# A macaron block on one core: block 2's down sum of the first FFN in sixteen steps, with six of the first attention round's scores between them

## The chip, the cores and the metric

The kernel runs on one core of one Trainium2 chip. A core has five engines, each with its own instruction queue: TensorE (PE, matrix products; its loading of weights is shown as PEld), VectorE (DVE), ScalarE (ACT), GpSimd (POOL) and SyncE (SP), which here only issues DMA transfers. PE writes its results to PSUM, from where DVE and ACT fetch them. The metric is the device time of one execution in microseconds; the time given for a kernel is the median over runs.

## What is computed

The reference is a macaron block over x of 2 sequences of 1024 tokens with 256 channels: half an FFN, attention, half an FFN again, each on a layer norm of x and added to x.

```python
x = x + 0.5 * ffn(layernorm(x), w_gate, w_up, w_down)
x = x + attn(layernorm(x), Wq, bq, Wk, bk, Wv, bv, Wo, bo)
x = x + 0.5 * ffn(layernorm(x), w_gate, w_up, w_down)

def ffn(x, w_gate, w_up, w_down):
    h = silu(x @ w_gate) * (x @ w_up)          # 1024 hidden
    h = keep_the_2_largest_of_each_4(h)        # by absolute value
    return h @ w_down
```

The attention has 32 query heads of size 8 on 8 key heads, rotary positions, a causal mask and a softmax.

## The kernel before

**Blocks and units.** The 2048 tokens are cut into four blocks of 512 (0 to 3; blocks 0 and 1 are the first sequence). The first FFN goes block by block: a layer norm and transpose, gate and up products (`gate_up`, L252), DVE's masks for the 2-of-4 choice (`mask`, L275 to L292, the last of which writes h), and the down sum. The down sum of a block (`down_half`, L297 to L316) is two halves of two tiles with eight matmuls each, 32 matmuls in all; the profile shows two records for each of them. The generator yields after every second matmul, so that a block has 16 steps of two matmuls. `down` runs a whole half per step of the plan; `down_slowly` gives the steps singly. A finished half is added to x either by DVE (`add`, L340) or by ACT and POOL (`add_aside`, L329 and L330).

Attention goes over 16 units, one for each sequence and key head. A unit's operands are made by `prepare`: PE transposes (hT, L529), ACT copies the result to stage (L537), and DMAs spread it into the tiles qT and kT (L550, L557) on rows that were cleared or set to one earlier. Only unit 0 uses the queues of SP and ACT, all others use SP alone. A unit is then worked in two passes. The first (`pass1`, L584 for the scores, L599 for the mask on the diagonal, L613 for DVE's maxima) finds the row maxima; they are split in two numbers by POOL (L415, L416), transposed (mT, L640), and copied by DMA into qT (L651). The second (`pass2`, L669) makes the scores once more, already shifted by the maxima, ACT takes the exponent (L679), POOL clears what lies above the diagonal (L685), and `weighted` (L706) multiplies with the values. A round interleaves the second pass of one unit with the first pass of the next; round 0 has the first pass of unit 0 only, 18 scores.

**Order.** The engines' order is written by hand where it matters. `run` follows a plan, a string of steps; PE's and DVE's instructions are issued just so. In it g is a group of gate and up products, m a part of a mask, d a half of a down sum, a an addition, l a part of a layer norm, and p one step of the attention's generator, which projects the first sequence and prepares unit 0. Rounds follow the string `order`; there PE and POOL keep the written order, and the other engines are ordered by a scheduler. PE executes in its written order: an instruction that waits holds up those behind it.

The plan of the first FFN ends with block 2's down sum and its two additions. Then the attention's generator goes on: it opens new pools in the space that the first FFN used, and clears there the qT and kT of two more units (`rows`, L397 and L400), which waits for that FFN's last readers. Round 0 follows, and beside its scores block 3's down sum, in steps of `down_slowly`: two steps at each odd one of the first twelve scores, and what is left at the end of the round. The score tiles are taken from `ps_big`, which has three buffers that go round among gate and up products, transposes hT and scores of both passes. The sums take one buffer of `ps_acc` and one of `ps_tr`; the latter serves mT too.

Of the kernel before, what the change touches and what calls it, by code (L numbers as in the profile page):

```python
# [35 lines left out]
def macaron_kernel(  # L36
# [23 lines left out]
    ps_tr = ctx.enter_context(tc.tile_pool(name="ps_tr", bufs=1, space=PSUM))  # L60
    ps_acc = ctx.enter_context(tc.tile_pool(name="ps_acc", bufs=1, space=PSUM))
# [161 lines left out]
    class FFN:  # L223
# [79 lines left out]
        def down_half(self, tb, t2, pool, tag):  # L303
# [11 lines left out]
                        yield  # L315
            self.adds.append((tb, t2, o))  # L316

        def down_slowly(self, tb):

            for t2 in range(2):  # L320
                yield from self.down_half(tb, t2, ps_acc, "acc")
                self.add_aside()
# [26 lines left out]
        def run(self, plan, gens, outs=()):  # L349

            make = {"g": self.gate_up, "d": self.down}
            with tc.manual_schedule(engines={mybir.EngineType.PE, mybir.EngineType.DVE}):
                for op in plan.split():
                    if op == "m":
                        if next(self.masks[0], 0) == 0:
                            self.masks.pop(0)
                    elif op == "a":
                        self.add()  # L360
                    elif op == "o":
                        if next(outs[0], 0) == 0:
                            outs.pop(0)
                            next(outs[0])
                    else:
                        if op not in gens:
                            tb = int(op[1])
                            gens[op] = (
                                make[op[0]](tb)
                                if op[0] in make  # L370
                                else layernorm_T(tb, lambda tb=tb: self.normed(tb), halves=tb == 0)
                            )
                        next(gens[op])

# [9 lines left out]
    def attention(actx, beside_first, beside_last, outs):  # L386
# [413 lines left out]
        def parsed(order):  # L800
            return [(op[0], *map(int, op[1:])) for op in map(str.split, order.split(";"))]

        ops = parsed(order)
        PAIRS = [("av", k) for k in (1, 3, 5, 7)]
        first = max(i for i, op in enumerate(ops) if op[0] == "p1" and op[1] < 3)
        units = [(b, g) for b in range(B) for g in range(NKV)]
# [4 lines left out]
        def step(op, prev, cur, nxt):  # L811
            kind, *arg = op
            if kind == "p1" and cur is not None:
                cur.pass1(*steps1[arg[0]], arg[1:] or (0, 1))
            elif kind == "p2" and prev is not None:
                es = prev.pass2(*steps2[arg[0]], arg[1:] or (0, 1))
                made.setdefault(arg[0], (prev, {}))[1].update(es)
            elif kind == "av" and arg[0] in made:
                unit, es = made.pop(arg[0])
                qh, kbs = steps2[arg[0]]  # L820
                last = arg[0] in (2, 9)
                unit.weighted(qh, kbs, es, last)
                if last and unit.g == NKV - 1:
                    outs.append(output(unit.b, qh))
                    next(outs[-1])
                    if unit.b < B - 1:
                        divisions.append(outs[-1])
            elif kind == "neg1" and prev is not None:
                prev.negated(1)
            elif kind == "shift":  # L830
                unit = prev if arg[0] == 1 else cur
                if unit is not None:
                    unit.shift(arg[0])
            elif kind == "prep" and nxt is not None:
                nxt.prepare()
# [5 lines left out]
        prev, cur = None, Unit(*units[0])  # L841
        cur.prepare()
        yield
        rctx = ExitStack()
        right = rctx.enter_context(tc.tile_pool(name="att2r", bufs=1, side="right"))
        rows(right)
# [7 lines left out]
        def a_step():  # L854
            while beside and next(beside[0], beside) is beside:
                beside.pop(0)

        def round_(n, prev, cur):
            nxt = Unit(*units[n + 1]) if n + 1 < len(units) else None
            if n == 1:  # L860
                beside.append(second)
            if nxt is not None and nxt.b == 1:
                for _ in second:
                    pass
            firsts = 0
            for i, op in enumerate(ops):
                step(op, prev, cur, nxt)
                if i == first and cur is not None:
                    cur.negated(0)
                if n == 0 and i == first:  # L870

                    nc.scalar.activation(warm, cur.maxima[0][:, 0, 6:7], AF.Exp, scale=0.0)
                if n == 0 and op[0] == "p1":
                    firsts += 1
                    if firsts <= 12:
                        for _ in range(2 * (firsts % 2)):
                            next(beside_first, None)
                if n > 0:
                    for _ in range(2 if op in PAIRS else op[0] in ("av", "prep")):
                        a_step()  # L880
                if n > NKV and op == ("av", 5) and divisions:
                    next(divisions.pop(0))
            return cur, nxt

        engines = {mybir.EngineType.PE, mybir.EngineType.Pool}
        with tc.tile_pool(name="att_round0", bufs=2, side="right") as late["2"]:
            with tc.manual_schedule(engines=engines):
                prev, cur = round_(0, prev, cur)
                for _ in beside_first:
                    pass  # L890
# [6 lines left out]
        with tc.manual_schedule(engines=engines):  # L897
            for n in range(1, len(units)):
                prev, cur = round_(n, prev, cur)
# [11 lines left out]
    with ExitStack() as fctx:  # L911
        actx = ExitStack()
        gens, outs = {}, []

        def second_starts():


            while not second:
                yield
            made = [outs.pop(0), outs.pop(0)]  # L920
            lns = [
                layernorm_T(tb, lambda tb=tb: second[0].normed(tb), copy=nc.vector.tensor_copy)
                for tb in range(2)
            ]

            for k in (0, 1):
                next(made[k])
            yield
            for gen in (made[0], made[0], lns[0], made[1], made[1], lns[0], lns[1], lns[0]):
                next(gen)  # L930
                yield
            for gen in (lns[1], lns[1]):
                next(gen)
                yield

        second = []
        with last_units:
            first = FFN(0, False, f0 := ExitStack(), wd_sb, last_pool)
            att = attention(actx, first.down_slowly(NTB - 1), second_starts(), outs)
            with f0:  # L940
                first.run(
                    """
                    l0 l0 l0 l1 g0 l1 g0 l2 g0 g0 l2 g0 m l1 g0 g0 l2 m g0 m g1 m g1 m g1 m
                    g1 g1 m g1 d0 m a d0 l3 a p g1 p g1 m g2 m p g2 m g2 m p p p g2 p d1 m m
                    g2 m d1 a a l3 g2 p g2 l3 p g2 m p g3 p p m g3 p p m g3 g3 g3 m g3 m g3
                    m g3 p m m m d2 d2 a a
                    """,
                    {"p": att},
                )
            next(att)  # L950
        next(att)
        early_ctx.close()
        second.append(FFN(1, True, fctx))
        for _ in att:
            pass
        second[0].run(
            """
            o g0 g0 g0 g0 m o g0 g0 o m g0 o g0 m g1 m g1 m g1 m g1 o g1 l2 g1 d0 m l2 g1 g1
            m m m l2 a d0 g2 m g2 o g2 g2 o m a g2 m o l3 g2 l3 g2 d1 m m g2 m m l3 d1 g3 m
            g3 g3 g3 a a g3 m g3 m g3 m g3 d2 m m m a d2 d3 a d3 a a  # L960
            """,
            gens,
            outs,
        )
        actx.close()
# [56 lines left out]
```

## Time and profile before

| what | us |
|---|---|
| median of 3 runs | 820.93 (820.42 to 822.25) |
| profiled execution, its own time | 824.67 |
| span of the profiled execution | 822.9 |
| PE busy (matmul) | 786.1, 96% of the span |
| DVE busy | 654.7, 80% |
| ACT busy | 426.9, 52% |
| POOL busy | 236.2, 29% |
| L613, DVE's maxima of scores, 288 of them | 343.2 |
| L307, PE's down sums, 512 records | 116.6 |

The span is the time from the first to the last recorded instruction, the profiled execution's own time contains what lies around it. Busy time is a mean over stages that are bound by different engines, so the stretch in which the change lies has to be read by itself: it reaches from about 166 us, where block 2's down sum begins, to about 211 us, where round 1 begins. Matmul records overlap, as they are pipelined: the time of a row of records is read from the start of the first to the start of what follows. The granted clock of PE is given as a share of full speed.

### The profile page before, as it was taken

How to read it: one execution, taken by the hardware profiler on the slowest of the kernel's cores; microseconds unless marked ns; L12 is line 12 of the kernel's file. 1: busy time of each engine (PE TensorE's matmuls, PEld its weight loads, DVE VectorE, ACT ScalarE, POOL GpSimd, SP SyncE). 2: the span in 40 equal slices, each digit the busy share in tenths (PEclk: the TensorE clock that was granted, in tenths of full speed). 3: DMA queues.
4: the chain of work that ended last, by engine and by line, in shares of the span. 5: the costliest groups of instructions: out<-in, count | busy, mean ns of one | idle time of the engine just before them, and what ended most of it. 6: DMA issues, size and time to landing. Idle time of an engine off the chain costs nothing.

```text
span 822.9 us, 13949 instructions
## 1 busy us (share of the span) xinstructions
PE 786.1 (96%) x5344; PEld 426.4 (52%) x5344; DVE 654.7 (80%) x871; ACT 426.9 (52%) x531; POOL 236.2 (29%) x443
## 2 busy tenths in 40 slices
PE   5999999998899999999999999999999999999998
PEld 2447574476544444454444444444445445657466
DVE  4797999898768796888888788888885479788692
ACT  1331313211677776877787687878877423122210
POOL 3000294821265465464222322233223100000000
PEclk9999999999999999999999899999999999999999
DMA  8100000022213222311333323322202200000001
GB/s 276 31 0 2 0 2 0 0 41 41 33 27 64 44 46 50 67 31 44 66 68 70 93 65 68 56 44 51 57 28 92 74 1 16 1 26 1 11 16 51
DMA packets 31010, 36.03 MB, mean 44 GB/s; under 512 B 12896, under 2 KB 20960, under 8 KB 30944
## 3 DMA queue, kind: packets, MB, share of 16 engines
q1 hardware_dynamic: 29118, 31.85, 17.2%
q10 hardware_dynamic: 1826, 3.29, 1.2%
q8 instruction: 42, 0.69, 0.4%
q14 instruction: 24, 0.20, 0.1%
HBM read 10.75 MB, written 10.75 MB: 26 GB/s over the span
## 4 chain that ended last, share of the span: by engine, by line
PE 71%; DVE 22%; ACT 4%; issue 1%; POOL 1%; DMA 0%; DVEq 0%; ACTq 0%
PE gu L252 20%; PE av L706 16%; PE s L584 9%; PE s L669 9%; PE o L307 9%; DVE maxima L613 8%; ACT e L679 3%; DVE h L292 2%; PE pr L474 2%; PE oo L753 2%; DVE h L262 1%; DVE sg L261 1%; DVE b L275 1%; PE s L599 1%; PE hT L529 1%
## 5 line engine op out<-in xcount | busy, mean ns | idle before, releaser
L613 DVE TENSOR_REDUCE maxima<-s 128x2 f32<-128x1024 f32 (+2 forms) x288 | 343.2, 1220 | 67.2 <-PE s L584 44.3
L679 ACT ACTIVATE e<-s 128x1024 f32<-128x1024 f32 x288 | 287.4, 1023 | 83.4 <-PE s L669 75.1
L706 PE MATMUL av<-e,vaug 128*32 128x512 f32 (+3 forms) x1536 | 158.5, 501 | 0.0
L685 POOL TENSOR_SCALAR_AFFINE_SELECT e<-e 128x256 f32<-128x256 f32 (+1 forms) x224 | 98.3, 451 | 201.5 <-ACT e L679 201.0
L584 PE MATMUL s<-kT,qT 64*128 64x512 f32 (+3 forms) x768 | 133.3, 386 | 14.6 <-ACT e L679 11.7
L669 PE MATMUL s<-qT,kT 64*128 64x512 f32 (+3 forms) x768 | 134.7, 395 | 3.1 <-DVE maxima L613 2.2
L252 PE MATMUL gu<-xnT,wg_sb 128*128 128x512 f32 x256 | 122.3, 600 | 0.7 <-ACT xnT L206 0.7
L252 PE MATMUL gu<-xnT,wu_sb 128*128 128x512 f32 x256 | 120.4, 593 | 0.0
L307 PE MATMUL o<-wd_sb,h 128*128 128x256 f32 x512 | 116.6, 386 | 0.9 <-DVE x L340 0.8
L584 PEld LDWEIGHTS s<-kT,qT 64*128 64x128 f32 x768 | 67.9, 187 | 82.7 <-ACT e L679 37.2
L307 PEld LDWEIGHTS o<-wd_sb,h 128*128 128x128 f32 x512 | 98.1, 193 | 18.5 <-issue 3.7
L669 PEld LDWEIGHTS s<-qT,kT 64*128 64x128 f32 x768 | 67.5, 186 | 62.1 <-DVE maxima L613 32.9
L260 ACT ACTIVATE sg<-gu 128x512 f32<-128x512 f32 x64 | 38.0, 593 | 113.6 <-PE gu L252 113.6
L263 ACT ACTIVATE a<-h 128x512 f32<-128x512 f32 x64 | 40.3, 630 | 104.9 <-DVE h L262 104.8
L252 PEld LDWEIGHTS gu<-xnT,wu_sb 128*128 128x128 f32 x256 | 48.9, 191 | 61.8 <-issue 61.8
L261 DVE TENSOR_TENSOR sg<-sg,gu 128x512 f32<-128x512 f32 x64 | 43.6, 681 | 46.1 <-ACT sg L260 46.0
L252 PEld LDWEIGHTS gu<-xnT,wg_sb 128*128 128x128 f32 x256 | 48.6, 192 | 54.6 <-issue 50.0
L181 POOL TENSOR_TENSOR rstd<-ve,neg_half 128x4 f32<-128x4 f32 x12 | 12.2, 1015 | 194.1 <-DVE ve L179 192.3
L706 PEld LDWEIGHTS av<-e,vaug 128*32 128x32 f32 x1536 | 34.1, 109 | 50.2 <-issue 38.8
L262 DVE TENSOR_TENSOR h<-sg,gu 128x512 f32<-128x512 f32 x64 | 43.9, 687 | 2.2
L599 PE MATMUL s<-half_id,half_mask 64*128 64x64 bf16 (+1 forms) x768 | 43.8, 205 | 0.0
L292 DVE SCALAR_TENSOR_TENSOR h<-w,h 128x512 f32<-128x512 bf16 x64 | 43.7, 743 | 0.0
(80 smaller groups left out, 562.4 us busy)
## 6 DMA issues: line engine op xcount, KB each, us to landing
avs<-oT SPq DMA_DIRECT2D x32, 256.0 KB
qT<-stage SPq DMA_DIRECT2D x124, 64.0 KB
kT<-stage SPq DMA_DIRECT2D x124, 32.0 KB
qT<-mrow SPq DMA_DIRECT2D x128, 4.0 KB
heads<-avs SPq DMA_DIRECT2D x16, 128.0 KB
out<-x SPq DMA_DIRECT2D x7, 256.0 KB
wu_sb<-in_wu SPq DMA_DIRECT2D x2, 512.0 KB
wg_sb<-in_wg ACTq DMA_DIRECT2D x2, 512.0 KB
```

The costliest lines, as they stand in the source:

```text
L252: nc.tensor.matmul(out=gu[:, i, :], lhsT=w_sb[:, kc, gb, j, :], rhs=self.xnT[tb][:, kc, :], start=(kc == 0), stop=(kc == 1),)
L261: nc.vector.tensor_tensor(sg, sg, gu[:, 0, :], ALU.mult)
L262: nc.vector.tensor_tensor(h[:, j, :], sg, gu[:, 1, :], ALU.mult)
L292: nc.vector.scalar_tensor_tensor(h[:, j, :], w[:, j, :], at, h[:, j, :], op, ALU.mult)
L307: nc.tensor.matmul(out=o[:, i, :], lhsT=self.hms[tb][k // 4][:, k % 4, bass.ts(2 * t2 + i, P)], rhs=self.wd_sb[:, k // 4, k % 4, :], start ...
L584: nc.tensor.matmul(out=to[:, i, s, bass.ds(col, n)], lhsT=self.qT[strip, pair, bass.ts(qt, P)].bitcast(FR), rhs=self.kT[strip, bass.ds(kc ...
L599: nc.tensor.matmul(out=last.rearrange("p (t n) -> p t n", n=P)[:, :, bass.ts(h, STRIP)], lhsT=half_mask[strip, h, :], rhs=half_id[strip, N ...
L613: ins = nc.vector.tensor_reduce(dst, src, AX.X, ALU.max, negate=True)
L669: nc.tensor.matmul(out=to[:, i, s, bass.ds(col, n)], lhsT=self.kT[strip, bass.ts(kb, P)].bitcast(FR), rhs=self.qT[strip, pair, bass.ds(q0, ...
L679: nc.scalar.activation(e, to, AF.Exp, scale=SCALE)
L685: nc.gpsimd.affine_select(out=first, in_=first, pattern=[[0, 2], [0, len(pairs)], [1, P]], compare_op=ALU.is_ge, fill=0.0, base=0, channel ...
L706: nc.tensor.matmul(out=self.av[32 * i : 32 * i + 32, TB - n : TB], lhsT=vaugs[self.b][:, kb, bass.ds(self.g * VW, 32)], rhs=es[i][:, bass. ...
```

## The change

Block 2's two plan steps d2 become steps of a new generator `down_finely`, which runs the same two halves in sixteen steps of two matmuls. Eleven of them stand at the place of d2, with the addition of the first half after the ninth. The others alternate with six steps p of the attention's generator, each of which now issues one of unit 0's first six scores (`HEAD`), before the pools of the next units are opened and their qT and kT cleared. The second half's addition follows behind the six. A seventeenth e2 only ends the generator; `next(gens[op], None)` allows that.

In round 0 those six scores are left out. After each of the other twelve stands one step of block 3's down sum, and after every fourth two; one step is left for the end of the round. Before, it was two steps after every other of the first twelve scores and four at the end. The matmuls, maxima, transfers and additions are the same ones in both kernels.

```diff
+        def down_finely(self, tb):
+
+            for t2, (pool, tag) in enumerate(((ps_acc, "acc"), (ps_tr, "tr"))):
+                yield from self.down_half(tb, t2, pool, tag)
+
...
-            make = {"g": self.gate_up, "d": self.down}
+
+            make = {"g": self.gate_up, "d": self.down, "e": self.down_finely}
...
-                        next(gens[op])
+                        next(gens[op], None)
...
         ops = parsed(order)
+        HEAD = 6
...
         cur.prepare()
         yield
+        scores = [op for op in ops if op[0] == "p1"]
+        for op in scores[:HEAD]:
+            step(op, prev, cur, None)
+            yield
         rctx = ExitStack()
...
             for i, op in enumerate(ops):
+                if n == 0 and op in scores[:HEAD]:
+                    continue
                 step(op, prev, cur, nxt)
...
                 if n == 0 and op[0] == "p1":
                     firsts += 1
-                    if firsts <= 12:
-                        for _ in range(2 * (firsts % 2)):
-                            next(beside_first, None)
+                    for _ in range(1 + (firsts % 4 == 0)):
+                        next(beside_first, None)
...
-                    m g3 p m m m d2 d2 a a
+                    m g3 p m m m e2 e2 e2 e2 e2 e2 e2 e2 e2 a e2 e2 p e2 p e2 p e2 p e2 p e2 p e2 a
```

## The prediction

> **What bounds the kernel here.** I read the page's chain of waits first: TensorE (PE) carries 71% of it and VectorE (DVE) 22%, so time lost on PE between the first FFN and the attention is lost for good. The timeline of the changed stretch shows where it is lost now:
>
> ```profile
> 166.42 14.03 PE L307 MATMUL o<-wd_sb,h 128*128 128x256 f32 x64
> ...
> 176.61 0.54 ACTq L557 DMA_DIRECT2D qT<-stage  x1
> ...
> 178.71 2.49 DVE L292 SCALAR_TENSOR_TENSOR h<-w,h 128x512 f32<-128x512 bf16 x4
> 180.37 0.51 PE L584 MATMUL s<-kT,qT 64*128 64x256 f32 x4
> ...
> 181.85 1.99 PE L307 MATMUL o<-wd_sb,h 128*128 128x256 f32 x8 [0.84 <-DVE x L340]
> ...
> 200.40 0.50 PE L584 MATMUL s<-kT,qT 64*128 64x512 f32 x2 [0.78 <-DVE maxima L613]
> ...
> 204.51 6.14 PE L307 MATMUL o<-wd_sb,h 128*128 128x256 f32 x16
> ```
>
> The first line is block 2's down sum: 64 records, that is 32 matmuls, 0.219 us a record, PE without a gap. Scores follow at 180.37. From 181.85 on, two scores and two steps (8 records) of block 3's down sum alternate. From 199.1 PE waits for DVE's maxima, and its last 16 records take 6.14 us where 16 x 0.219 = 3.5 would do. Round 1 starts at 210.58 with PE's first exponent score, right behind that sum; this is the moment to compare.
>
> Why the last sum is slow is in the table of windows (busy PE after the width, then PEld, DVE, ACT, POOL, then the granted clock):
>
> ```profile
> 178.72:182.13 3.41, 2.57 (x21) 1.91 (x21) 3.41 (x7) 0.00 (x0) 1.57 (x1) 1.00 0.00 0
> 199.20:202.61 3.41, 1.42 (x8) 0.37 (x4) 3.41 (x4) 0.00 (x0) 0.00 (x0) 1.00 0.14 24
> 202.61:206.02 3.41, 3.27 (x14) 2.21 (x15) 3.41 (x4) 0.00 (x0) 0.00 (x0) 0.50 0.02 5
> 206.02:209.43 3.41, 3.41 (x10) 2.69 (x9) 1.32 (x3) 0.00 (x0) 0.00 (x0) 0.50 0.00 0
> ...
> 305.01:308.42 3.41, 2.73 (x24) 1.36 (x22) 3.41 (x5) 2.23 (x3) 2.31 (x5) 1.00 0.51 78
> ...
> 462.02:465.43 3.41, 2.18 (x25) 1.61 (x25) 3.41 (x4) 2.81 (x4) 1.40 (x5) 1.00 0.31 86
> ```
>
> The clock falls to 0.50 three times, after each of the windows with 1.42, 2.73 and 2.18 us of busy PE, and comes back one or two windows of 3.41 us later (at 209.43, 311.83 and 472.25). The first window shows that 2.57 us, mostly of the dense down sum, still holds it.
>
> The changed path also needs two more things: when the first unit's operands have landed (busy share of the DMA engines is the last figure but one), and what a change between down sum and scores costs (the chain in order of time):
>
> ```profile
> 177.50:178.00 0.50, 0.50 (x4) 0.45 (x3) 0.50 (x2) 0.00 (x0) 0.00 (x0) 1.00 0.65 98
> 178.00:178.50 0.50, 0.50 (x4) 0.45 (x3) 0.50 (x3) 0.00 (x0) 0.00 (x0) 1.00 0.21 41
> 178.50:179.00 0.50, 0.50 (x4) 0.42 (x4) 0.50 (x2) 0.00 (x0) 0.00 (x0) 1.00 0.00 0
> ```
>
> ```profile
> 188.07 1.92 PE o L307 x8
> 190.00 0.43 PE s L584 x2
> 190.42 0.07 PE s L599 x4
> 190.50 0.32 PE s L584 x2
> 190.81 0.07 PE s L599 x4
> ```
>
> Eight records ought to take 8 x 0.219 = 1.75; they take 1.92. Leaving the 128-row sum for the 64-row scores costs 0.17. The first score of a pair costs 0.50, the second 0.39.
>
> **A new wait on PE: +2.4.** In the new plan eleven of block 2's sixteen steps stand ahead of the first score: 11 x 4 x 0.219 = 9.6, so PE reaches that score at 166.42 + 9.6 = 176.05. The instruction order of the changed kernel shows that it waits for all copies of stage into qT and kT. They don't move: stage is copied at 168.90 and the last one is issued at 176.61 on ACT's queue, held there behind an Abs that waits for DVE. The DMA engines fall still within 178.0 to 178.5. I take 178.45 for the score's start. Behind it in PE's order stand the other five steps, which could have run but may not pass. Before, the same landing was hidden under the rest of the 14.03.
>
> **Head, 178.45 to 186.85.** Six scores alone: 0.60 (the diagonal one with eight mask matmuls), 0.43 (no mask), 0.56, 0.50, 0.56, 0.50 = 3.15. Five single steps: 4 x 0.219 + 0.17 = 1.05 each, 5.25. DVE does not stop them: its masks end at 181.20, one add (0.64) follows, and six maxima of 1.16 end at 183.0 ... 188.9, the fourth score needing only the first of them (three score buffers). The second add ends at 189.5.
>
> **Round 0 after the head.** The transpose hT 0.57 (chain: 186.56 to 187.13) and 0.2 until the fifth maximum frees the next score's buffer: 187.6. Twelve scores: 0.43 x 7 + 0.50 x 2 + 0.56 x 2 + 0.60 = 5.7. Block 3's sixteen steps: nine singles 9.45, two pairs 3.84, the last three together 2.8 = 16.1. The transpose mT 0.45. mT waits for POOL: the memsets of the next units' qT and kT wait for the last matmul of block 2's sum (before: 180.56, with 17.96 us of idle POOL ahead of them). That matmul now ends near 186.4; the four memsets take 5.3, and with the cast, the vaug memset that now stands between (0.73) and the subtraction, ms is ready at about 193.0. PE is there at 192.3: +0.7. DVE has 1.5 us per score and needs 1.16, so the tail no longer waits for it and its clock drop goes.
>
> Sum: 187.6 + 5.7 + 16.1 + 0.45 + 0.7 = **210.6, against 210.58 before**. By differences: the wait at 181.14 (0.7) and the tail's excess (199.4 to 210.58 is 11.2 for 1.85 of scores and 3.5 of steps: 5.8) go; the DMA wait (2.4), ten more changes (1.7), scores alone instead of paired (about 1.1), and the waits for POOL and a buffer (0.9) come. That is 6.5 against 6.1, even within the 0.5 us that the rounded rows allow.
>
> Edits at nothing: the stage copy of unit 1 now stands behind the warming exponent on ACT, waiting for DVE until about 188.0, but hT itself ends at 187.4. Its SP DMAs, eighteen with the zeros at about 0.65, wait for kT1's memset (189.4) and end near 201.2, then the four mrow DMAs near 203.8 (before 201.3). Cover: round 1 needs them at 210.6; if that cover were gone, about 2.5. The added matmul records are none; the same sums are done.
>
> **Whether the clock falls in the new wait.** Here the Trainium skill ("TensorE: Matmul & The Clock Gate", HAM oscillation) speaks of idle gaps of more than about 3.4 us. A gap of 2.4 would be safe by that: +0.0. The row 199.20:202.61 above fell without any single gap over 0.8; it was the sum over the window that was short. By the rows, a window that holds the wait whole has about 1 us of busy PE and must fall. If a window's edge cuts the wait in the middle, both halves may hold as the row of 178.72 did. Taking the edge's place as unknown from one execution to the next, and 70% of dense work after the wait, the clock falls for some 7 edges in 10. The trace's three drops lasted two windows, one, and two. One half-clock window of PE-bound work costs 3.41 x (1 - 0.219/0.43) = 1.67 (0.43: of the last sum's 16 records, 4.5 fit behind 209.43 at 0.219, so 11.5 took the 4.92 us before it). Bounds: 0 and 3.3. I take between one and two windows, 2.5, less 0.1 of the small buffer wait that it covers: **+2.4**. I follow the row.
>
> Everything after round 0 is unchanged in order, so the shift is passed on whole. The profiled execution took 824.67 with a span of 822.9; the median of the runs shown is 820.93. I add the difference to the median: **823.3**.
>
> **Cases.**
> 1. Forecast (0.58): wait for the DMAs, clock falls. 822.0 to 824.8.
> 2. Wait, but the clock holds (0.31): even, 820.9, or 820 to 822 with the roundings. For it: the cut-window phases and the row of 178.72. Against: three drops in this trace with PE far from a long gap.
> 3. On the other side (0.11): the single steps cost no extra. If weight loads of the next form run under the mask matmuls, ten changes (1.7) and the lone scores (1.1) vanish; with the clock held, 818.1. It decides if a lone step's spacing is below 0.95. Against it: every eight-record chunk between scores in the trace shows 1.92.
> 4. That the plan does not lay the scores between the steps is excluded by the instruction order; that unit 1's DMAs arrive late and hold up round 1 (up to +2.5, 823.4) has 6 us of slack against it and lies inside case 1's number.
>
> About 0.2% (1.6 us) is what a measurement can tell from no change. Most of case 1 lies beyond it and nearly all of case 2 within: slower 0.55, same 0.34, faster 0.11. The range 819.8 to 825.0 leaves out most of case 3 and the far end of a two-window drop.
>
> **What would show it.** In the new trace PE has a hole at about 176.0 to 178.5 ending on a DMA; the granted clock is 0.50 for one or two windows near 178 to 186 and 1.00 around 203 to 209; mT waits for POOL; round 1's first exponent score starts at 211 to 214. It is wrong if the hole is under 1.5 us, if lone steps take under 0.95, or if the tail still waits for maxima.

## The result, and the profile after

The changed kernel took 826.51 us in the median of six executions (823.96 to 829.33), the kernel before 821.49 beside it: a ratio of 1.0063, with a 95% interval of 1.0048 to 1.0078. It is slower by 5.0 us, about twice the forecast of 2.4, and lies above the range (825.0).

The timeline of the changed stretch in the new profile (start, duration, engine, line; in brackets the idle time ahead and what ended it; L590, L646 and L675 are the scores, mT and the exponent scores that were L584, L640 and L669):

```profile
167.30 9.71 PE L307 MATMUL o<-wd_sb,h 128*128 128x256 f32 x44
...
178.00 0.35 PE L590 MATMUL s<-kT,qT 64*128 64x256 f32 x1 [0.98 <-DMA kT<-stage]
...
179.60 0.84 PE L590 MATMUL s<-kT,qT 64*128 64x256 f32 x3 [1.25 <-DMA kT<-stage]
...
180.60 2.08 PE L307 MATMUL o<-wd_sb,h 128*128 128x256 f32 x4
...
191.14 1.81 POOL L403 MEMSET qT<- 128x2048 f32 x1 [27.65 <-PE o L307]
...
197.53 0.41 PE L646 MATMUL mT<-ident_r,ms 128*8 128x128 f32 x4 [0.53 <-POOL ms L422]
...
212.56 2.86 PE L307 MATMUL o<-wd_sb,h 128*128 128x256 f32 x12
...
215.34 0.50 PE L675 MATMUL s<-qT,kT 64*128 64x512 f32 x2
```

The hole is where it was forecast, and DMA ends it: PE is through with the eleven steps at about 176.9 (167.30 + 44 x 0.219), one record of the first score gets through at 178.00, the other three start at 179.60. So PE waits about 2.7 us for its operands (176.9 to 179.6). A lone step right after it, four records, lasts 2.0 us instead of 1.05. At the other end the last twelve records take 2.8 at full speed, where before sixteen took 6.1. In the profile of before, round 1's first exponent score is

```profile
210.58 0.50 PE L669 MATMUL s<-qT,kT 64*128 64x512 f32 x2
```

From the start of block 2's sum to round 1's first exponent score it is 215.34 - 167.30 = 48.04, against 210.58 - 166.42 = 44.16 before. I call this the stretch; it is 3.9 longer.

The table of windows shows the clock (busy PE after the width, the granted clock third from the end):

```profile
176.66:180.08 3.42, 1.09 (x5) 0.41 (x4) 3.42 (x8) 1.28 (x1) 0.00 (x0) 1.00 0.44 79
180.08:183.49 3.41, 3.40 (x16) 2.03 (x17) 3.41 (x6) 0.00 (x0) 0.00 (x0) 0.54 0.00 0
183.49:186.90 3.41, 3.41 (x14) 2.20 (x15) 1.97 (x3) 0.00 (x0) 0.00 (x0) 0.50 0.00 0
186.90:190.31 3.41, 3.41 (x24) 2.29 (x23) 2.26 (x3) 0.00 (x0) 0.00 (x0) 0.96 0.00 0
```

In this execution the hole fell nearly whole into one window, 1.09 of 3.42 us busy, and the clock was then halved: the 0.54 and the 0.96 in the rows put the drop at 180.35 to 187.2. All drops that lie inside the spans of these profiles last a whole multiple of 3.41 us (this one two, the longest four); I call each such piece a half-clock window.

Two further differences are not the change's. Block 2's sum starts 0.9 later here, a delay that is already there in the first 17 us, at the first gate and up products; the same kernel's second profile starts the sum at 166.42 like before. And each profile has other clock drops in the attention rounds: three windows in that of before (308 to 312, 465 to 472), one in this one (450 to 453). From round 1 to the second FFN's first product it is 433.4 before and 430.6 here, with the same instructions, 1.4 for each of the two windows of difference. So the spans of the profiles (822.9 and 825.0) say less than the stretch and the medians. The profile of before, from which the forecast was made, lost more clock than is usual for that kernel: it took 824.67 us at a mean clock of 0.990, with five half-clock windows, where its medians lie at 820.4 to 821.5 and most of its executions have a mean clock of 0.994 to 0.998. The changed kernel's profile (826.70, 0.994) is close to its median.

### The profile page after: what moved, and what is told of

It is laid out like the page before. It is cut to its first block, busy times and chain, and to the rows that moved or that the text cites. A ratio compares the mean times of both kernels' runs of the same rounds, so it can differ in the third digit from the quotient of the medians.

```text
span 825.0 us, 13950 instructions
## 1 busy us (share of the span) xinstructions
PE 788.0 (96%) x5344; PEld 425.4 (52%) x5344; DVE 655.9 (80%) x871; ACT 426.5 (52%) x531; POOL 236.2 (29%) x443
## 4 chain that ended last, share of the span: by engine, by line
PE 72%; DVE 20%; ACT 4%; DMA 1%; issue 1%; POOL 1%; SPq 0%; DVEq 0%; ACTq 0%; POOLq 0%
PE gu L252 20%; PE av L712 16%; PE s L590 9%; PE s L675 9%; PE o L307 9%; DVE maxima L619 8%; ACT e L685 3%; PE pr L480 2%; DVE h L292 2%; PE oo L759 2%; DVE h L262 1%; DVE sg L261 1%; PE s L605 1%; PE hT L535 1%; PE lnT L202 1%
## 5 line engine op out<-in xcount | busy, mean ns | idle before, releaser
L590 PE MATMUL s<-kT,qT 64*128 64x512 f32 (+3 forms) x768 | 134.5, 385 | 14.6 <-ACT e L685 11.6
L675 PE MATMUL s<-qT,kT 64*128 64x512 f32 (+3 forms) x768 | 134.4, 394 | 3.2 <-DVE maxima L619 2.2
L307 PE MATMUL o<-wd_sb,h 128*128 128x256 f32 x512 | 119.2, 388 | 0.3 <-ACT half L334 0.3
L590 PEld LDWEIGHTS s<-kT,qT 64*128 64x128 f32 x768 | 68.1, 186 | 85.7 <-ACT e L685 37.0
L675 PEld LDWEIGHTS s<-qT,kT 64*128 64x128 f32 x768 | 66.9, 184 | 61.6 <-DVE maxima L619 33.0
L181 POOL TENSOR_TENSOR rstd<-ve,neg_half 128x4 f32<-128x4 f32 x12 | 12.2, 1016 | 195.0 <-DVE ve L179 193.0
```

The source lines that it names most:

```text
L307: nc.tensor.matmul(out=o[:, i, :], lhsT=self.hms[tb][k // 4][:, k % 4, bass.ts(2 * t2 + i, P)], rhs=self.wd_sb[:, k // 4, k % 4, :], start ...
L590: nc.tensor.matmul(out=to[:, i, s, bass.ds(col, n)], lhsT=self.qT[strip, pair, bass.ts(qt, P)].bitcast(FR), rhs=self.kT[strip, bass.ds(kc ...
L675: nc.tensor.matmul(out=to[:, i, s, bass.ds(col, n)], lhsT=self.kT[strip, bass.ts(kb, P)].bitcast(FR), rhs=self.qT[strip, pair, bass.ds(q0, ...
```

## The experiments

Four theories. **A**: the hole brings a clock drop, and half clock is the larger part of the loss. **B**: the loss is the wait itself and the many changes between 128-row sum and 64-row scores; the clock is a side effect. **C**: round 0's new spacing is what costs. **D**: round 0 is bound by DVE's maxima, whatever PE does. The stretch is read from each profile; "windows" counts the half-clock windows inside it. The ratio weighs all executions of both kernels; it is not the quotient of the two medians beside it.

| kernel | stretch, us | windows | median, us | before beside it | ratio, 95% interval |
|---|---|---|---|---|---|
| before (first profile) | 44.16 | 2, at the tail | 821.49 | | |
| changed | 48.04 | 2, at the head | 826.51 | 821.49 | 1.0063 (1.0048 to 1.0078) |
| changed, again | 50.77 | 4, at the head | 826.64 | 821.24 | 1.0062 (1.0037 to 1.0087) |
| hole filled | 44.86 | 0 | 821.77 | 820.38 | 1.0006 (0.9995 to 1.0017) |
| new head, old pairs | 45.38 | 2, at the head | 822.32 | 820.38 | 1.0015 (1.0006 to 1.0024) |
| new spacing alone | 42.93 | 0 | 825.03 | 820.38 | 1.0043 (1.0028 to 1.0057) |
| late head | 44.72 | 1, behind the head | 824.94 | 820.38 | 1.0041 (1.0026 to 1.0056) |
| one score in the hole | 48.03 | 1 at the head, 2 at the tail | 824.53 | 821.24 | 1.0029 (1.0013 to 1.0044) |
| hole filled, old pairs | 42.34 | 0 | 819.71 | 821.24 | 0.9978 (0.9968 to 0.9989) |
| pairs to the end | 39.28 | 0 | 819.70 | 821.24 | 0.9968 (0.9956 to 0.9981) |
| pairs to the end, again | 39.24 | 0 | 818.02 | 820.55 | 0.9965 (0.9954 to 0.9976) |
| pairs, earlier addition | 38.31 | 0 | 818.30 | 820.55 | 0.9960 (0.9947 to 0.9972) |

### The hole filled

```diff
-            def pass1(self, tiles, at, pairs):
+            def pass1(self, tiles, at, pairs, fill=0):
...
+                for _ in range(fill):
+                    nc.tensor.matmul(
+                        out=sc[:, 0, 0:C],
+                        lhsT=wg_sb[:, 0, 0, 0, :],
+                        rhs=wu_sb[:, 0, 0, 0:2, :],
+                        start=True,
+                        stop=True,
+                    )
...
-        for op in scores[:HEAD]:
-            step(op, prev, cur, None)
+        for i, op in enumerate(scores[:HEAD]):
+            if i == 0:
+                cur.pass1(*steps1[op[1]], op[2:] or (0, 1), fill=6)
+            else:
+                step(op, prev, cur, None)
```

The throwaway results go into the score's own buffer and are overwritten.

> The changed kernel with six throwaway matmuls (12 records, 12 x 0.219 = 2.6 us) ahead of the first score's own, in the hole where PE waits for the DMAs. Theory A (the clock falls because of the hole, and half clock over two windows is the larger part of the loss): no drop near 180 to 187, some 3.3 us less than the changed kernel, about 823. Theory B (the loss is the wait itself and the changes between down sum and scores; the clock costs little): within 0.7 of the changed kernel, 826 to 827.

PE's timeline, filled:

```profile
176.44 2.75 PE L583 MATMUL s<-wu_sb,wg_sb 128*128 128x256 f32 x12
179.12 0.84 PE L598 MATMUL s<-kT,qT 64*128 64x256 f32 x4
179.62 0.48 PE L613 MATMUL s<-half_id,half_mask 64*128 64x64 bf16 x8
180.03 1.13 PE L307 MATMUL o<-wd_sb,h 128*128 128x256 f32 x4
181.09 0.50 PE L598 MATMUL s<-kT,qT 64*128 64x512 f32 x2
```

Its windows (columns as above):

```profile
176.66:180.08 3.42, 3.42 (x25) 2.61 (x23) 3.42 (x9) 1.28 (x1) 0.00 (x0) 1.00 0.34 64
180.08:183.49 3.41, 3.41 (x21) 2.23 (x21) 3.41 (x6) 0.00 (x0) 0.00 (x0) 1.00 0.00 0
```

The first score starts hardly earlier than in the changed kernel (12.2 us after the start of block 2's sum, 12.3 there), yet the clock never drops in this profile, the stretch is 3.2 shorter, and the ratio to before has 1 inside its interval. So 3.2 of the 3.9 by which the stretch had grown go with the drop; the wait as such stayed, and B falls. The median fell further than A expected (821.77 against about 823). The changed kernel's most frequent mean clock, 0.994, stands for three half-clock windows (each takes 0.002 off the mean), and its first profile has the third at 450 to 453, where this profile has none; why, no run shows. Lone steps at full clock take 1.06 (180.03 to 181.09) and lone scores 0.43, as forecast.

### The parts alone

New head, with the spacing of round 0 as before:

```diff
-                    for _ in range(1 + (firsts % 4 == 0)):
-                        next(beside_first, None)
+                    if firsts <= 12:
+                        for _ in range(2 * (firsts % 2)):
+                            next(beside_first, None)
```

> The head of the changed kernel, with round 0's remaining scores beside two steps of block 3 at every other one, as before. Theory A (hole and clock): both stay; six changes fewer save 6 x 0.17 and six paired scores 6 x 0.1, so 1.3 to 1.6 less than the changed kernel, about 825. Theory C (the loss sits in round 0's new spacing): close to before, 821 to 822.

The 822.32 is nearer to C's figure than to A's, which is a miss in size. Hole and drop stay, and the stretch is 2.7 shorter than the changed kernel's at the same two windows; with the hole filled, the same edit ("hole filled, old pairs" below) saves 2.5. So the new spacing is a cost beside the drop and not much smaller: the old pairs alone take the ratio from 1.0063 to 1.0015, the filled hole alone takes it to 1.0006. The pairs save the waits of mT for POOL (0.53) and of a step for ACT's copy of the accumulator (0.26), which the changed kernel has; the other 1.7 to 1.9 are its lone steps and scores, to which I gave 1.3 to 1.6.

The spacing alone: the kernel before with the new rule for all 18 scores.

```diff
-                    if firsts <= 12:
-                        for _ in range(2 * (firsts % 2)):
-                            next(beside_first, None)
+                    for _ in range(1 + (firsts % 4 == 0)):
+                        next(beside_first, None)
```

> Block 2's down sum in one piece as before, all 18 scores in round 0 with the new spacing of block 3's steps. Theory A: no hole, no drop at the head; the sixteen steps are used up at the 13th score, the last five scores go at DVE's pace of 1.16, round 1 starts 1 to 2 us earlier than before: 819 to 821. Theory C (the spacing is what costs): slower than before, 823 to 826.

A's number is a miss: 825.03. Its end of round 0 on PE:

```profile
205.52 0.96 PE L584 MATMUL s<-kT,qT 64*128 64x512 f32 x6
207.34 0.50 PE L584 MATMUL s<-kT,qT 64*128 64x384 f32 x4 [0.86 <-DVE maxima L613]
...
208.47 0.49 PE L584 MATMUL s<-kT,qT 64*128 64x512 f32 x2 [0.51 <-DVE maxima L613]
209.60 0.55 PE L669 MATMUL s<-qT,kT 64*128 64x512 f32 x2 [0.64 <-DVE maxima L613]
```

Round 1 does start 1.2 earlier, as A said, but the last five scores have no step left beside them and PE waits for maxima again. The clock is half from 209.9 to 220.2, three windows, now inside round 1, and four of its six executions have a mean clock of 0.990. The number fits C, but the stretch is 1.2 shorter than before's, so the loss lies behind it, in the clock: from round 1 to the second FFN's first product its profile has five half-clock windows and takes 434.9, against 429.1 to 429.3 in the four profiles that have none there. Lone steps are not free here either: with pairs to the end of round 0 (below) the stretch is another 3.7 shorter.

### Where the first score stands

Late head: fourteen steps ahead of the first score.

```diff
-                    m g3 p m m m e2 e2 e2 e2 e2 e2 e2 e2 e2 a e2 e2 p e2 p e2 p e2 p e2 p e2 p e2 a
+                    m g3 p m m m e2 e2 e2 e2 e2 e2 e2 e2 e2 a e2 e2 e2 e2 e2 p e2 p e2 p e2 p p p a
```

> The changed kernel with fourteen steps of block 2's sum ahead of the first score instead of eleven (two between the scores, the last three scores one behind the other). PE reaches the first score 2.6 us later, at the landing. Theory A: hole under 1 us, no clock drop, 4.5 to 5.5 less than the changed kernel: 821 to 822. Theory B (changes between sum and scores are the loss): three changes fewer, 0.8 less, 825 to 826.

The hole is gone and the stretch is 3.3 shorter than the changed kernel's, where B gave 0.8. But the median fell only to 824.94: A's 821 to 822 is missed, and B's 825 to 826 almost met. Its scores four to six wait for maxima (0.20, 0.56, 0.51, and hT 0.56), and the clock fell behind them, from 187.8 to 191.2. So one hole was traded for four smaller ones. The profiled execution was the quickest of seven (822.16, mean clock 0.997); the others had 0.992 or 0.993, so they lost more windows than it shows. Where, no profile shows: that stays open.

One score alone in the hole, the other five steps behind it in one piece, then the old pairs in round 0 (that part of the edit is the one shown for the new head):

```diff
-        HEAD = 6
+        HEAD = 1
...
-                    m g3 p m m m e2 e2 e2 e2 e2 e2 e2 e2 e2 a e2 e2 p e2 p e2 p e2 p e2 p e2 p e2 a
+                    m g3 p m m m e2 e2 e2 e2 e2 e2 e2 e2 e2 a e2 e2 p e2 e2 e2 e2 e2 e2 a
```

> Only the first score is drawn into block 2's sum, after eleven steps; the other five steps follow it in one piece, and round 0 is spaced as before (pairs). Theory A: the DMA hole alone brings its clock drop: two windows of half clock at the head (3.3) and part of the hole (2.4), less what the tail's wait for DVE takes up, 823 to 826. Theory B (the many changes are the loss): one change more than before, within 1 of it.

824.53, inside A's range and 2.3 above the upper end of B's. The hole alone drops the clock; with hardly a change more than before, the kernel is slower. Its windows at the head (same columns):

```profile
176.76:180.17 3.41, 1.29 (x10) 0.72 (x9) 3.41 (x9) 0.00 (x0) 0.00 (x0) 0.99 0.41 73
180.17:183.58 3.41, 3.41 (x16) 2.71 (x13) 3.41 (x6) 0.00 (x0) 0.00 (x0) 0.51 0.00 0
183.00:186.40 3.40, 3.40 (x16) 2.80 (x14) 0.73 (x1) 0.00 (x0) 0.00 (x0) 0.93 0.00 0
```

Here the drop lasts one window (the last row overlaps the one above it; its 0.93 ends the drop at about 183.5), while 20 records of the down sum run in one piece.

### The changed kernel once more

> The changed kernel once more, for more executions beside the kernel before on one chip. By theory A (hole, clock lost for about two windows, the changes between sum and scores) 3.9 more than before from the trace of the stretch, 3.5 to 5.5; by the forecast's even case less than 1.

```profile
175.11:178.52 3.41, 1.37 (x6) 0.75 (x4) 3.41 (x8) 1.24 (x1) 0.00 (x0) 0.99 0.60 108
178.52:181.94 3.42, 3.25 (x17) 2.08 (x17) 3.42 (x7) 0.04 (x1) 0.00 (x0) 0.50 0.00 0
181.94:185.35 3.41, 3.41 (x13) 2.05 (x14) 2.13 (x2) 0.00 (x0) 0.00 (x0) 0.50 0.00 0
185.35:188.76 3.41, 3.41 (x17) 1.98 (x16) 1.41 (x2) 0.00 (x0) 0.00 (x0) 0.50 0.00 0
188.76:192.18 3.42, 3.42 (x14) 2.21 (x14) 1.68 (x2) 0.00 (x0) 0.00 (x0) 0.51 0.00 0
192.18:195.59 3.41, 3.41 (x30) 2.20 (x28) 2.93 (x5) 1.21 (x2) 2.61 (x2) 1.00 0.02 5
```

The same program, the same hole, but four half-clock windows, and a stretch of 50.77. The two more cost 2.73, 1.4 each. The eight executions agree: they range from 823.60 at a mean clock of 0.998 to 831.41 at 0.986. One half-clock window is 1.7 of 825 us, or 0.002 of the mean, so these are six windows apart for 7.8 us, 1.3 each. The profiles of all versions give a third count, as they run the same instructions from round 1 to the second FFN's first product: 429.1 to 429.3 without a half-clock window there (four profiles), 430.5 and 430.6 with one, 431.8 and 431.9 with two, 432.8 to 433.5 with three, 434.9 with five, so 1.1 to 1.4 each.

The kernel before ran beside it on that chip. At a mean clock of 0.998 its executions took 820.1 to 820.7 against 823.6 for the changed one, at 0.994 822.2 to 823.8 against 826.3 and 827.0, at 0.990 824.6 to 825.2 against 828.4 and 828.8. So at the same number of lost windows the changed kernel is some 3 to 4 us slower, about what its first profile's stretch says with two windows on either side. In the profiles it does not so much add a drop as move it, from the tail of round 0 to the head, and it pays the hole and the lone steps in exchange for the tail's waits.

### Versions that keep PE busy

Filled hole and old pairs together:

> The head of the changed kernel with the hole filled by six throwaway matmuls and round 0 in pairs as before. Theory A: no clock drop at head or tail; 45.4 (head alone in pairs) less 3.3, so about 42 us from the start of block 2's sum to round 1 against 44.2 before: 818 to 819. Theory B: as the head alone in pairs, about 822.

819.71, above A's 818 to 819, but 0.22% below before (0.11% to 0.32%), though it runs 2.6 us of throwaway work. Its stretch is 3.0 shorter than the new head with pairs: two windows again, 1.5 each.

The kernel before, without the limit to twelve scores:

```diff
                     firsts += 1
-                    if firsts <= 12:
-                        for _ in range(2 * (firsts % 2)):
-                            next(beside_first, None)
+                    for _ in range(2 * (firsts % 2)):
+                        next(beside_first, None)
```

> The kernel before with one condition gone: two steps of block 3's sum at every other score of all 18, not of the first twelve, so that no steps are left over and no score goes alone. Theory A (a PE that stays busy keeps its clock): no wait for maxima and no clock drop near 200 to 210, round 1 starts about 3 us earlier, 817 to 819. Theory D (round 0 is bound by DVE's 18 maxima whatever PE does): the same as before, within 1.

PE's end of round 0 there:

```profile
202.19 1.99 PE L307 MATMUL o<-wd_sb,h 128*128 128x256 f32 x8
204.12 0.73 PE L584 MATMUL s<-kT,qT 64*128 64x512 f32 x6
204.69 0.29 PE L599 MATMUL s<-half_id,half_mask 64*128 64x128 bf16 x4
204.79 0.48 PE L584 MATMUL s<-kT,qT 64*128 64x512 f32 x2
205.94 0.50 PE L669 MATMUL s<-qT,kT 64*128 64x512 f32 x2 [0.67 <-DVE maxima L613]
```

No wait for maxima inside round 0, no sum left over, no drop: the stretch is 4.9 shorter than before. Of that 2.6 us arrive in the ratio (0.32% of 821), and 1.5 between the two medians; 819.70 is just above A's 817 to 819. Round 1 then waits for DVE, and the clock falls there, from 209.8 to 216.6 in this profile, which takes a part back. D falls, as the interval lies wholly below it (1 us is 0.12%).

> The kernel with pairs of steps at all odd scores once more, on another chip: 0.2 to 0.45% below before by theory A; within 0.1% by theory D.

0.35% below before: the same.

With DVE's first addition ahead of the last part of the masks:

```diff
-                    m g3 p m m m d2 d2 a a
+                    m g3 p m m d2 a m d2 a
```

> The same, with DVE's addition of block 2's first half moved ahead of the last part of its masks, so that PE need not wait 0.85 for the accumulation buffer at 182. If PE sets round 0's end, 0.7 to 0.9 less than the pairs alone; if the end is set by DVE's maxima by now, no difference (within 0.3).

PE no longer waits at 182 (the step behind the first score starts at 181.19, not 182.10), the stretch shrinks by 0.9, and the median by nothing: 818.30 against 818.02. The executions that kept a clock of 0.999 or more took 815.3 to 816.1, those of the pairs alone 816.8 to 817.6; but most lost it, and here the drop began at 206.9 and lasted three windows, where in the pairs' second profile it had been two from 209.4. The gain is there and is given back as clock. Both versions beat both kernels.

## Why the prediction was wrong in size

**Right.** The new wait on PE, its place and its cause; that it halves the clock, against the rule of a longer gap that the prediction quotes (all four profiles that have the hole show the drop, and none of the fourteen executions of the changed kernel kept a mean clock above 0.998); that the tail's wait for maxima and its drop go; mT's new wait for POOL (0.53, forecast 0.7); the price of a lone step (1.06, forecast 1.05) and of a lone score. From behind hT to round 1 the sum said 22.95 and the trace 23.16 (192.18 to 215.34). The third case, lone steps without extra cost, is excluded by those 1.06.

**Wrong: the length of the clock drop.** The step reads "I take between one and two windows, 2.5 [...] +2.4". The bound it gave was 3.3, from the one or two windows that before's three drops had lasted. The changed kernel's two profiles show two and four windows. Against the filled hole's 44.86 that is 3.2 (48.04) and 5.9 us (50.77). The price of one window was near, 1.4 to 1.6 against 1.67; the count was not. What sets the count stays open. Lone steps and lone scores followed the hole in the three profiles with 2, 4 and 2 windows, and the down sum in one piece in the profile with 1, which looks as if thinner work held the clock down. Other drops say otherwise: behind the late head's waits stood a transpose, a lone score and a lone step, and its drop lasted one window; the tail's drops, before and with one score in the hole, lasted two, though in each the second window held nothing but the down sum.

Two windows alone would not have left the range: 820.93 + 3.9 is 824.8. The rest of the 5.0 that the medians show, about 1.1, is not in the first profile's stretch. The forecast added the shift of one profile to the median, and that profile, of before, has more half-clock windows than most of its executions; whether before loses two windows at the tail in each execution, as the forecast's saving there assumes, no run shows.

**Smaller: the even case was 0.7 too low.** Without a drop the stretch is 44.86, not 44.2. Of that, about 0.5 is the first score: with the hole filled it starts 12.2 us after the sum's start where I had 12.0 (0.3 more in the changed kernel, so a hole of 2.7, not 2.4), and takes 0.91 (179.12 to 180.03) where I had 0.60. Another 0.26 is a wait that the working has not: the second half of block 3's sum needs the one buffer that ACT copies, and ACT comes to it later than PE (205.59).

Together, 0.7 and 3.2 to 5.9 make the 3.9 to 6.6 by which the stretch is longer than before; the medians differ by 5.0 and 5.4. The round-0 spacing, which the forecast only counted as changes, is a part of its own: 2.5 us of the stretch with the clock held (44.86 against 42.34).

## What to carry to other kernels

A hole on TensorE is priced twice: by its own length (2.7 us here) and by the half-clock windows after it (3.2 to 5.9), and here the second was the larger. Before work is put between other work, look at when its data land, and put work that needs nothing in the hole; but look then at what waits next: the late head closed the hole, got new waits for DVE in exchange, and stayed 0.41% above before. Interleaving in single pieces has a price too: here pairs were 2.5 us cheaper with the clock held. A change that removes a wait can be worth nothing where PE then waits elsewhere and loses its clock, as after the earlier addition, so the granted clock belongs beside every comparison of two profiles.

## What was not expected of the hardware

Half clock can last through windows in which PE's records show it busy almost without a break: four in a row in the second profile of the changed kernel, each with 3.25 to 3.42 us of busy PE. So busy time of PE in the profile does not by itself bring the clock back, and what does is open. The same program's executions lay 7.8 us apart on one chip by the number of such windows alone, as far as their mean clocks tell (0.998 to 0.986).
